# A state-space scan and two mixtures of experts on one core: rows stored once per token, a first stage in written order, and other loads behind the scan

## The chip, the core and the metric

The kernel runs on one core of a Trainium2 chip. Five engines work side by side and wait for one another on semaphores: TensorE (PE, matmuls, with its weight loads shown as PEld), VectorE (DVE), ScalarE (ACT), GpSimd (POOL) and SyncE (SP), which here only issues transfers. Sixteen DMA engines move the data; the queues that feed them belong to SP, ACT and POOL. The metric is the device time of one execution in microseconds (us), lower is better.

## What is computed

x has 8 sequences of 1024 tokens with 256 channels, 8192 tokens in all. Cut to what matters, the reference is:

```python
xn = layernorm(x)
x  = x + scan_block(xn) + routed_experts(xn) + shared_expert(xn)
xn = layernorm(x)
x  = x + attention(xn) + capacity_experts(xn)

def scan_block(x):      # per channel a state of 16: h = A h + Bm x_t; y_t = Cm h + Dm x_t
    return x + gelu(layernorm(y, ln_w, ln_b)) @ W_out.T + b_out
def routed_experts(x):  # 8 experts of width 128, 2 per token, chosen in one of two groups
    # sum over the 2 of  weight * (silu(x @ w_gate) * (x @ w_up)) @ w_down
    ...
def attention(x):       # softmax over the axis of heads; with one head every weight is 1
    # so each token of a sequence gets the same row: the sum of all values, times w_o
    ...
def capacity_experts(x):  # 8 experts of width 1024, 2 per token, at most 2048 tokens per expert
    ...
```

## The kernel before

The work is tiled by 128 tokens (`P`): 64 tiles (`NT`), 8 per sequence (`TPB`), 8 sequences (`NB`). Tensors between the stages lie in DRAM: `xnd` (the normalized rows with the weight of their expert), `base` (x plus normalized x plus shared expert plus b_out), `yr` (what the routed experts give, two rows per token), `xd` (second normalized rows), and the output.

A planner puts the instructions of each engine in an order of its own, by the order in which the code names them as priority, by estimated durations, and by when buffers of a pool come free. The order is fixed when the program is built; each engine then works through its list and waits where an operand is missing. The transfers of SP's and POOL's queues are in such lists too.

**First stage** (lines 457 to 660). For each tile DVE takes mean and variance (`measure`, L553, L554), ACT the root (`scale`, L561), DVE the normalized rows (`normal`, L576). Four tiles of rows make one buffer `xr4` (three buffers), which goes to `xnd` twice, once for each of the two rows that a token has there (L584). `shared` (L596) takes two tiles at a time: PE transposes the rows (`pair_turned`, L249), ACT copies them (L253), PE forms the router's scores (L606) and the shared expert's gate and up products (L263); ACT writes the normalized channels `xc` for the scan and x plus xn into `y` (`both`, L588, L592) and the sigmoid (L268); DVE multiplies (L270, L271), PE goes down (L278), DVE adds the result into `y` (L617). For each sequence `fill` (L535) first writes b_out to all rows of `base`, and POOL adds the finished `y` to it in an accumulating transfer (L655). For every two sequences `route0` chooses the experts (33 small DVE operations) and writes the two weights to `xnd` (L528). The tiles are measured in five sets (1, 2, 2, 2 and 1 sequences), the next set while one is worked on. The eight steps of `krylov(0)` (powers of the first scan matrices) are called two per pair. PE's PSUM buffers are `ps_t` (1), `ps_m` (2), `ps_k` (2, shared by krylov and every second pair's gate/up), `ps_gu` (1), `ps_d` (1).

**Scan and routed experts** (L662 to L902). Eight blocks of channels; under the first two, `find` sorts tokens into 71 expert blocks of 256 rows, `found` (L757) decodes for each row which token and which of its two experts it is; under the other six the blocks run: `bring` gathers rows and weights (L789, L792), `widen` and `narrow` compute, `narrow` scales with the row's weight (L811) and scatters to `yr` (L814).

**Behind the scan** (L905 to L1336). Per sequence: `load(b)` (L942) brings `base` into `hb` (three buffers) and adds the two rows per token of `yr`: for sequence 0 by plain loads into the two buffers `xs` and DVE adds (L959, L961), for the others by two accumulating transfers on POOL's queue (L952), the second behind the first. `turn`, `project` (L988, PE L996, DVE L1003 adds `hb`), `measure`, `normal_out`, `turn_out`, `logits`, `attend`, `route` follow. `attend` (L1071) computes the attention's one row and POOL adds it to all rows of the sequence in the output (L1085). The first two experts' weights `w1t` are loaded in this stage (L909).

**Last experts** (L1339 to L1432). 32 steps of 512 rows: gather (`fetch`, L1362), two layers (PE L1393, L1411), and four scatters per step that add to the output (L1423), each waiting for the one before.

The loop of the first stage that the change rewrites:

```python
for k in range(0, len(g), 2):
    ...
    shared(i, pr, rstd[:, k : k + 2])
    for step in steps[:2]:
        step()
```

Of the kernel before, what the change touches and what calls it, by code (L numbers as in the profile page):

```python
# [9 lines left out]
F32 = mybir.dt.float32  # L10
# [8 lines left out]
P = 128  # L19
EPS = 1e-5  # L20
BIG = 3.0e38


@with_exitstack
def kernel(
# [47 lines left out]
    NCOL = NBLK * BLK // P  # L73
    XW = D + 8
# [10 lines left out]
    kscr = dram.tile([D, 2 * P], F32, name="kscr")  # L85
    base = dram.tile([NTOK, D], F32, name="base")

    xnd = dram.tile([2 * NTOK, D + 1], F32, name="xnd")
# [109 lines left out]
    def pick_two(pool, v, n, hot, val):  # L198


        for k in range(2):
# [6 lines left out]
            nc.vector.tensor_reduce(first, cand, AX.X, ALU.max)  # L208
            oh = hot[k]
            nc.vector.tensor_tensor(oh, cand, bc(first, 2, [P, n, E]), ALU.is_equal)  # L210
            if k == 0:
                rest = pool.tile([P, n, E], F32, name="rest")
                nc.vector.scalar_tensor_tensor(rest, oh, -BIG, v, ALU.mult, ALU.add)
                v = rest


    with tc.tile_pool(name="xpool", bufs=1) as xpool, tc.tile_pool(name="mo", bufs=2) as mo, tc.tile_pool(
# [12 lines left out]
        g0 = xpool.tile([P, 2, NT], F32, name="g0")  # L230
        up = xpool.tile([P, NT], F32, name="up")
        off = xpool.tile([P, NT], F32, name="off")
# [4 lines left out]

        choice = xpool.tile([P, NCOL], I32, name="choice")
        goes = xpool.tile([P, NCOL], I32, name="goes")
# [16 lines left out]
        def hidden(xT, wb, pgu=None):  # L256
# [10 lines left out]
            sg = mo.tile([P, 2 * P], F32, name="sg")  # L267
            nc.scalar.activation(sg, pgu[:, 0, :], AF.Sigmoid)  # L268
            hh = mo.tile([P, 2 * P], F32, name="hh")
            nc.vector.tensor_tensor(hh, pgu[:, 0, :], sg, ALU.mult)  # L270
# [183 lines left out]
        with tc.tile_pool(name="sh", bufs=1) as sh, tc.tile_pool(name="ld", bufs=2) as ld, tc.tile_pool(  # L454
# [5 lines left out]
            scores = sh.tile([P, NT, E], F32, name="scores")  # L460
            cb_t = sh.tile([P, E], F32, name="cb_t")
# [10 lines left out]
            bout_t = sh.tile([P, D], F32, name="bout_t")  # L472
            nc.scalar.dma_start(bout_t, b_out.partition_broadcast(P))
# [6 lines left out]
            nc.vector.tensor_copy(rwT.rearrange("p c e -> p (c e)"), pr[:, : DC * E])  # L480

            def route0(n, tiles):
# [8 lines left out]
                nc.vector.tensor_tensor(lo, v[:, :, 0:2], v[:, :, 2:4], ALU.min)  # L491
                gs = rt.tile([P, 2 * n], F32, name="gs")
                nc.vector.tensor_reduce(gs, lo, AX.X, ALU.max)
                top = rt.tile([P, 2 * n], F32, name="top")
                nc.vector.tensor_reduce(top, hi, AX.X, ALU.min)
                nc.vector.tensor_tensor(gs, gs, top, ALU.max)
                nc.vector.tensor_reduce(top, hi, AX.X, ALU.max)
                nc.vector.tensor_tensor(gs, gs, top, ALU.add)
                gs2 = gs.rearrange("p (t g) -> p t g", g=2)
                gm = rt.tile([P, n, 2], F32, name="gm")  # L500
                nc.vector.tensor_tensor(gm[:, :, 0], gs2[:, :, 0], gs2[:, :, 1], ALU.is_ge)
                nc.vector.tensor_tensor(gm[:, :, 1], gs2[:, :, 1], gs2[:, :, 0], ALU.is_gt)
                masked = rt.tile([P, n, E], F32, name="masked")
# [7 lines left out]
                pick_two(rt, masked, n, hot, [rt.tile([P, n], F32, name=f"top{j}") for j in range(2)])  # L511
                w = rt.tile([P, n, E], F32, name="w")
                nc.vector.tensor_tensor(hot0[:, tiles, :], hot[0], hot[1], ALU.add)
                nc.vector.tensor_copy(first0[:, tiles, :], hot[0])
                nc.vector.tensor_tensor(w, hot0[:, tiles, :], sc, ALU.mult)
                den = rt.tile([P, n], F32, name="den")
                nc.vector.tensor_reduce(den, w, AX.X, ALU.add)
                nc.vector.tensor_scalar(den, den, 1e-20, None, ALU.add)
                nc.vector.reciprocal(den, den)
                nc.vector.tensor_tensor(w, w, bc(den, 2, [P, n, E]), ALU.mult)  # L520
                for k in range(2):
                    wk = rt.tile([P, n, E], F32, name="wk")
                    nc.vector.tensor_tensor(wk, w, hot[k], ALU.mult)
                    nc.vector.tensor_reduce(g0[:, k, tiles], wk, AX.X, ALU.add)
                    mine = xnd[2 * tiles.start * P : 2 * tiles.stop * P, :].rearrange(
                        "(i p k) c -> k p i c", p=P, k=2
                    )[k]
                    nc.sync.dma_start(mine[:, :, D], g0[:, k, tiles])  # L528
# [4 lines left out]
            def fill(b):  # L533

                nc.sync.dma_start(  # L535
                    base[b * S : (b + 1) * S, :].rearrange("(i p) d -> p i d", p=P),
                    bc(bout_t, 1, [P, TPB, D]),
                )

# [31 lines left out]
            def normal(i, mv, rstd):  # L571
# [7 lines left out]
                if i % 4 == 3:  # L579
                    for kk in range(2):  # L580
                        mine = xnd[2 * (i - 3) * P : 2 * (i + 1) * P, :].rearrange(
                            "(i p k) c -> k p i c", p=P, k=2
                        )[kk]
                        nc.sync.dma_start(mine[:, :, :D], rows[i // 4])  # L584
# [10 lines left out]

            def shared(i, pr, rstd):  # L596


                n = i // 2
                pt = None  # L600
                if n % 3:
                    pt = ps_m.tile([P, 512], F32, name="pm").rearrange("p (c t) -> p c t", c=DC)
                xT = pair_turned(rows[i // 4][:, i % 4 : i % 4 + 2, :], pt)
# [11 lines left out]
                pgu = ps_k.tile([P, 2, 2 * P], F32, name="pk") if n % 2 else None  # L615
                pd = down(hidden(xT, sw, pgu), sw)
                nc.vector.tensor_tensor(y[:, i : i + 2, :], pd, y[:, i : i + 2, :], ALU.add)  # L617

# [7 lines left out]
            pr = None  # L626
            for s, g in enumerate(sets):
                mv = mvs[s]
                rstd = scale(g, mv)
                nxt = []  # L630
                if s + 1 < len(sets):
                    nxt = list(sets[s + 1])
                    mvs.append(ld.tile([P, len(nxt), 2], F32, name="mv"))
                for i in g[:4]:
                    normal(i, mv[:, i - g[0], 0:1], rstd[:, i - g[0] : i - g[0] + 1])
                for k in range(0, len(g), 2):
                    for i in g[k + 4 : k + 6]:
                        normal(i, mv[:, i - g[0], 0:1], rstd[:, i - g[0] : i - g[0] + 1])
                    for i in nxt[k * len(nxt) // len(g) : (k + 2) * len(nxt) // len(g)]:
                        measure(i, mvs[s + 1][:, i - nxt[0], :])  # L640
                    i = g[k]
                    if i % TPB == 0:
                        pr = ps_y.tile([P, TPB, E], F32, name="py")
                        fill(i // TPB)
                        if i // TPB >= NB - len(pack):
                            nc.sync.dma_start(*pack[i // TPB - NB + len(pack)])
                    shared(i, pr, rstd[:, k : k + 2])
                    for step in steps[:2]:
                        step()
                    steps = steps[2:]  # L650
                    if i % TPB == TPB - 2:
                        b = i // TPB
                        tiles = slice(b * TPB, (b + 1) * TPB)
                        nc.scalar.activation(scores[:, tiles, :], pr, AF.Sigmoid)
                        nc.gpsimd.dma_start(  # L655
                            base[b * S : (b + 1) * S, :].rearrange("(i p) d -> p i d", p=P),
                            y[:, tiles, :], accum_op=ALU.add,
                        )
# [807 lines left out]
```

## Time and profile before

| what | us |
|---|---|
| median of three runs (2046.37 to 2051.86) | 2048.63 |
| the profiled execution | 2030.81 |
| its span, first to last instruction | 2029.1 |
| PE busy | 1825.1 |
| ACT busy | 716.2 |
| DVE busy | 697.3 |
| POOL busy | 670.8 |
| last add of the shared expert ends (L617) | 203.3 |
| first load behind the scan (L946) | 858.3 |
| first gather of the last experts (L1362) | 1092.5 |

The profile is of one execution. Its page cuts the span into 40 slices of 50.7 us, each digit the busy share in tenths. A timeline line has start, duration, engine, source line, operation, output and inputs, the number of merged instructions, and in brackets how long the engine sat idle and for whom it waited. The chain of work that ended last is followed back from the last instruction. A granted clock of 1.00 is PE at full speed. In the diff, load_first(0) is given the two xs buffers as room, load_first(1) the two w1t buffers.

### The profile page before, as it was taken

To read this page: it belongs to the slowest core of one execution; us is meant where nothing else is said; L and a number is where in the kernel's file an instruction comes from. 1 tells how busy PE (TensorE), PEld (TensorE's weight loads), DVE (VectorE), ACT (ScalarE), POOL (GpSimd) and SP (SyncE) were. 2 spreads that over 40 slices of the span, in tenths; PEclk is the share of its full clock that TensorE was granted. 3 is DMA by queue.
4 is the path that set the end of the run, shared out by engine and by line. 5 is a ranking of instruction groups with operands and counts; after the bars stand their busy time and mean duration, and the time that the engine had idled before them with its cause. 6 is when DMAs were issued, how large, how long until landed. Compare 5 with 4: busy or idle time off the path is not lost.

```text
span 2029.1 us, 24196 instructions
## 1 busy us (share of the span) xinstructions
PE 1825.1 (90%) x8619; PEld 1379.9 (68%) x8619; DVE 697.3 (34%) x2101; ACT 716.2 (35%) x1626; POOL 670.8 (33%) x680
## 2 busy tenths in 40 slices
PE   6988798989898888748995999999999999999996
PEld 5866576877777776537973666666666666666664
DVE  6764795444453434437775111001000110001010
ACT  5963353232222222337982222222222222222221
POOL 0000002555555546411112333333333333333312
PEclk9988899999999999868997999999999999999998
DMA  9999313555454545499995223232323222232211
GB/s 267 222 199 201 49 54 115 151 149 152 146 164 138 146 130 170 122 281 253 224 237 128 38 60 61 42 72 39 82 39 73 41 61 57 57 59 38 40 18 21
DMA packets 228888, 233.16 MB, mean 115 GB/s; under 512 B 50904, under 2 KB 203296, under 8 KB 228640
## 3 DMA queue, kind: packets, MB, share of 16 engines
q0 software_dynamic: 69408, 102.87, 26.2%
q1 hardware_dynamic: 156672, 126.35, 22.5%
q10 hardware_dynamic: 2688, 2.40, 0.4%
q8 instruction: 68, 1.11, 0.2%
q14 instruction: 52, 0.43, 0.1%
HBM read 136.87 MB, written 97.85 MB: 116 GB/s over the span
## 4 chain that ended last, share of the span: by engine, by line
PE 48%; DMA 4%; issue 2%; DVE 2%; ACT 1%; POOL 1%; POOLq 0%; SPq 0%; DVEq 0%; ACTq 0%
PE phe L1393 22%; PE poe L1411 21%; DMA hb<-yr 2%; PE px L1376 1%; PE pd L996 1%; PE pd L1061 1%; DMA hb<-base 1%; PE pt L933 1%; DMA out_dram<-yo,invi 1%; PE pi L1162 0%; PE pt L1206 0%; PE pt L1042 0%; DVE y L1003 0%; DVE st L178 0%; POOL out_dram L1085 0%
## 5 line engine op out<-in xcount | busy, mean ns | idle before, releaser
L1393 PE MATMUL phe<-xTe,w1t 128*128 128x512 f32 x1024 | 447.1, 595 | 0.6 <-issue 0.6
L1411 PE MATMUL poe<-w2t,hT 128*128 128x256 f32 x2048 | 447.3, 379 | 0.0
L1411 PEld LDWEIGHTS poe<-w2t,hT 128*128 128x128 f32 x2048 | 386.7, 190 | 51.7 <-issue 0.5
L1393 PEld LDWEIGHTS phe<-xTe,w1t 128*128 128x128 f32 x1024 | 195.4, 191 | 233.6 <-issue 230.5
L1423 POOL DMA_INDIRECT out_dram<-yo,invi x128 | 201.6, 1575 | 447.7 <-DMA out_dram<-yo,invi 257.2
L1400 ACT ACTIVATE hT<-phe,b1T 128x512 f32<-128x512 f32 x256 | 175.9, 687 | 248.3 <-PE phe L1393 241.4
L1422 ACT ACTIVATE yo<-yo,gr 128x256 f32<-128x256 f32 x128 | 58.0, 500 | 441.4 <-DVE yo L1418 441.4
L1418 DVE TENSOR_TENSOR yo<-poe,b2t 128x512 f32<-128x512 f32 x64 | 44.2, 691 | 406.6 <-PE poe L1411 406.6
L1362 POOL DMA_INDIRECT xg<-xd,invi x128 | 124.0, 969 | 163.8 <-PE px L1376 125.8
L322 PE MATMUL pk<-kr 128*128 128x129 f32 (+7 forms) x896 | 151.4, 306 | 29.4 <-ACT kr L333 23.8
L1377 DVE COPY xTe<-px 128x512 f32<-128x512 f32 x64 | 41.2, 685 | 383.3 <-PE px L1376 383.2
L322 PEld LDWEIGHTS pk<-kr 128*128 128x128 f32 x896 | 130.1, 202 | 52.9 <-ACT kr L333 34.5
L814 POOL DMA_INDIRECT yr<-yo,goes x142 | 140.7, 990 | 76.7 <-DVE yo L811 35.2
L792 POOL DMA_INDIRECT xb<-xnd,choice x142 | 139.1, 980 | 46.9 <-issue 33.5
L263 PE MATMUL pgu<-xT,wb 128*128 128x256 f32 x568 | 144.2, 399 | 8.9 <-ACT xT L253 7.6
L263 PEld LDWEIGHTS pgu<-xT,wb 128*128 128x128 f32 x568 | 110.3, 200 | 37.4 <-ACT xT L253 18.5
L333 ACT COPY kr<-pk 128x256 f32<-128x256 f32 x192 | 69.6, 374 | 123.4 <-DVE kr L329 103.5
L268 ACT ACTIVATE sg<-pgu 128x256 f32<-128x256 f32 x87 | 33.3, 383 | 199.7 <-PE pgu L263 139.3
L278 PE MATMUL pd<-wb,hh 128*128 128x256 f32 x284 | 86.4, 421 | 11.4 <-DVE hh L271 7.6
L787 POOL COPY wb<-wrow 1x1 int32<-1x1 int32 x71 | 12.8, 180 | 234.4 <-PE pgu L752 117.5
L270 DVE TENSOR_TENSOR hh<-pgu,sg 128x256 f32<-128x256 f32 x87 | 36.8, 423 | 138.8 <-ACT sg L268 116.1
L996 PE MATMUL pd<-woutT,gT 128*128 128x256 f32 x256 | 63.5, 404 | 22.1 <-DVE y L1003 22.1
(322 smaller groups left out, 2375.3 us busy)
## 6 DMA issues: line engine op xcount, KB each, us to landing
wb<-wpk SPq DMA_DIRECT2D x71, 384.0 KB
xnd<-xr SPq DMA_DIRECT2D x32, 512.0 KB
hk<-kscr SPq DMA_DIRECT2D x32, 512.0 KB
hb<-yr POOLq DMA_DIRECT2D x14, 1024.0 KB
base<-bout_t SPq DMA_DIRECT2D x8, 1024.0 KB
base<-y POOLq DMA_DIRECT2D x8, 1024.0 KB
hb<-base SPq DMA_DIRECT2D x8, 1024.0 KB
w1t<-in_L_ffn_w_dram SPq DMA_DIRECT2D x8, 1024.0 KB
```

Source lines behind the costliest of these rows:

```text
L263: nc.tensor.matmul(pgu[:, j, :], lhsT=gu[:, j, c, :], rhs=xT[:, c, :], start=(c == 0), stop=(c == DC - 1),)
L278: nc.tensor.matmul(pd[:, q, :], lhsT=hh[:, q * P : (q + 1) * P], rhs=wb[:, 2 * DC * I : WW], start=True, stop=True,)
L322: nc.tensor.matmul(pk[:, j, :n], lhsT=t[:, 1 - j, P:], rhs=t[:, j, P - k : P - k + n], start=True, stop=True,)
L333: nc.scalar.copy(t[:, :, P:], pk[:, :, k : k + P])
L792: nc.gpsimd.indirect_dma_start(out=xb[:, q, : D + 1], out_offset=None, in_=xnd[:, :], in_offset=bass.IndirectOffsetOnAxis(ap=choice[:, 2 * ...
L814: nc.gpsimd.indirect_dma_start(out=next(yr_own)[:, :], out_offset=bass.IndirectOffsetOnAxis(ap=goes[:, 2 * n + q : 2 * n + q + 1], axis=0) ...
L996: nc.tensor.matmul(po[:, q, :], lhsT=gT[:, c, (t + q) * P : (t + q + 1) * P], rhs=woutT[:, c, :], start=(c == 0), stop=(c == DC - 1),)
L1362: nc.gpsimd.indirect_dma_start(out=xg[:, q, :], out_offset=None, in_=xd[:, :], in_offset=bass.IndirectOffsetOnAxis(ap=invi[:, q0 + q : q0 ...
L1393: nc.tensor.matmul(ph, lhsT=w1t[:, c, h * P : (h + 1) * P], rhs=xT[:, c], start=(c == 0), stop=(c == DC - 1),)
L1400: nc.scalar.activation(hT[:, h], ph, AF.Relu, bias=b1T[:, e * HC + h : e * HC + h + 1])
L1411: nc.tensor.matmul(po[:, r, :], lhsT=hT[:, h, q + r, :], rhs=w2t[:, h, :], start=(h == 0), stop=(h == HC - 1),)
L1423: nc.gpsimd.indirect_dma_start(out=of[:, :], out_offset=bass.IndirectOffsetOnAxis(ap=invi[:, q0 + r : q0 + r + 1], axis=0), in_=yo[:, r, : ...
```

## The change

*Rows.* `xnd` holds one row per token: 256 channels and both weights (258 numbers). The rows are written once. The routed experts' gather takes the whole row; `found` keeps in `which` which of the two weights is meant, and `narrow` picks it with a multiplication and a sum and adds half of b_out to each of a token's two rows (`bhalf`). So `fill` goes, and `base` is written by plain transfers of four tiles from SP's queue instead of accumulated.

*Written order.* In the first stage PE, DVE and ACT run in the order of the code. The code is staggered: transposes one pair ahead, the way down one pair behind, rows two pairs ahead, krylov's steps one every second pair, `route0` cut into pieces of which three run per pair. At a set's end, `begin(s + 1)` (root, scalings, four tiles of rows of the next set) stands ahead of the last pair's own work.

*Behind the scan.* Sequences 0 and 1 are loaded plainly, sequence 1's two halves into the buffers of `w1t`, and DVE adds them (`add_first`, two tiles at a time); `load(2)` is called at once. `attend` leaves its row in `y`, and POOL adds it to the output after one of the first eight steps of the last experts.

The diff, cut to its core:

```diff
+IN_ORDER = {mybir.EngineType.PE, mybir.EngineType.DVE, mybir.EngineType.Activation}
+    XR = D + 2
-    xnd = dram.tile([2 * NTOK, D + 1], F32, name="xnd")
+    xnd = dram.tile([NTOK, XR], F32, name="xnd")
...
+        bhalf = xpool.tile([P, D], F32, name="bhalf")
+        nc.scalar.dma_start(bhalf, b_out.partition_broadcast(P))
+        nc.scalar.mul(bhalf, bhalf, 0.5)
+        which = xpool.tile([P, NCOL, 2], BF16, name="which")
...
-            sg = mo.tile([P, 2 * P], F32, name="sg")
-            nc.scalar.activation(sg, pgu[:, 0, :], AF.Sigmoid)
-            hh = mo.tile([P, 2 * P], F32, name="hh")
-            nc.vector.tensor_tensor(hh, pgu[:, 0, :], sg, ALU.mult)
+            hh = mo.tile([P, 2 * P], F32, name="hh", bufs=3)
+            nc.scalar.activation(hh, pgu[:, 0, :], AF.Sigmoid)
+            nc.vector.tensor_tensor(hh, pgu[:, 0, :], hh, ALU.mult)
...
-                    for kk in range(2):
-                        mine = xnd[2 * (i - 3) * P : 2 * (i + 1) * P, :].rearrange(
-                            "(i p k) c -> k p i c", p=P, k=2
-                        )[kk]
-                        nc.sync.dma_start(mine[:, :, :D], rows[i // 4])
+                    mine = token_rows(slice(i - 3, i + 1))
+                    nc.sync.dma_start(mine[:, :, :D], rows[i // 4])
...
+            def add_shared(i, hh):
+                pd = down(hh, sw)
+                nc.vector.tensor_tensor(y[:, i : i + 2, :], pd, y[:, i : i + 2, :], ALU.add)
+                if i % 4 == 2:
+                    nc.sync.dma_start(
+                        base[(i - 2) * P : (i + 2) * P, :].rearrange("(i p) d -> p i d", p=P),
+                        y[:, i - 2 : i + 2, :],
+                    )
...
+            with tc.manual_schedule(engines=IN_ORDER):
+                begin(0)
+                turn(0)
+                pr, back = None, None
+                routes = {2 * TPB: 0, 4 * TPB: 2 * TPB, 6 * TPB: 4 * TPB, 7 * TPB: 6 * TPB, 8 * TPB: 7 * TPB}
+                routing = iter(())
+                for s, g in enumerate(sets):
+                    ...
+                    for k in range(0, len(g), 2):
+                        for i in g[k + 4 : k + 6]:
+                            mean, rstd, j = scale_of[i]
+                            normal(i, mean, rstd[:, j : j + 1])
+                        for i in nxt[k * len(nxt) // len(g) : (k + 2) * len(nxt) // len(g)]:
+                            measure(i, mvs[s + 1][:, i - nxt[0], :])
+                        if nxt and k == len(g) - 2:
+                            begin(s + 1)
+                        i = g[k]
+                        ...
+                        if i + 2 < NT:
+                            turn(i + 2)
+                        rstd = scale_of[i][1]
+                        hh = shared(i, pr, rstd[:, k : k + 2])
+                        if back:
+                            add_shared(*back)
+                        back = i, hh
+                        if i // 2 % 2 and steps:
+                            steps.pop(0)()
+                        for _ in range(3):
+                            next(routing, None)
+                        if i + 2 in routes:
+                            for _ in routing:
+                                pass
+                            routing = route0(i + 2 - routes[i + 2], slice(routes[i + 2], i + 2))
+                add_shared(*back)
...
+                gk = mo.tile([P, 2, 2], F32, name="gk")
+                tc.keep_in_program_order(nc.vector.tensor_tensor(
+                    gk, xb[:, :, D:XR], which[:, 2 * n : 2 * n + 2, :], ALU.mult
+                ))
+                gs = mo.tile([P, 2], F32, name="gs")
+                nc.vector.tensor_reduce(gs, gk, AX.X, ALU.add)
                 yo = eb_.tile([P, 2, D], F32, name="yo", bufs=2)
                 for q in range(2):
-                    nc.vector.tensor_scalar(
-                        yo[:, q, :], pd[:, q, :], xb[:, q, D : D + 1], None, ALU.mult
+                    nc.vector.scalar_tensor_tensor(
+                        yo[:, q, :], pd[:, q, :], gs[:, q : q + 1], bhalf, ALU.mult, ALU.add
                     )
...
+        def load_first(b, room):
+            hb = xr.tile([P, TPB, D], F32, name="hb")
+            nc.sync.dma_start(hb, base[b * S : (b + 1) * S, :].rearrange("(i p) d -> p i d", p=P))
+            parts = []
+            for h in range(2):
+                yk = room[h].rearrange("p (i k d) -> p i k d", k=2, d=D)
+                nc.sync.dma_start(yk, stored(b)[:, h * TPB // 2 : (h + 1) * TPB // 2])
+                parts.append(yk)
+            hold[b] = hb
+            return parts
+        def add_first(b, parts):
+            hb = hold[b][0] if isinstance(hold[b], tuple) else hold[b]
+            for t in range(0, TPB, 2):
+                at = t % (TPB // 2)
+                for j in range(2):
+                    nc.vector.tensor_tensor(
+                        hb[:, t : t + 2, :], hb[:, t : t + 2, :],
+                        parts[t * 2 // TPB][:, at : at + 2, j, :], ALU.add,
+                    )
...
-            at = rt.tile([P, D], F32, name="at")
-            nc.scalar.copy(at, pa[:, :D])
-            mine = of[b * S : (b + 1) * S, :].rearrange("(i p) d -> p i d", p=P)
-            nc.gpsimd.dma_start(mine, bc(at, 1, [P, TPB, D]), accum_op=ALU.add)
+            nc.scalar.copy(y[:, b * TPB, :], pa[:, :D])
...
-        load(0)
-        load(1)
+        firsts = [load_first(0, ...), load_first(1, ...)]
+        load(2)
         turn(0)
         measure_scan(0)
+        add_first(0, firsts[0])
...
                 roots(b)
+                if b == 0:
+                    add_first(1, firsts[1])
...
+                if n <= NB:
+                    nc.gpsimd.dma_start(
+                        of[(n - 1) * S : n * S, :].rearrange("(i p) d -> p i d", p=P),
+                        bc(y[:, (n - 1) * TPB, :], 1, [P, TPB, D]), accum_op=ALU.add,
+                    )
```

## Prediction

> **What bounds the kernel now.** I read the page's slices, then stretches of the span, the queues' shares, the chain, and the timelines of PE, DVE, ACT and POOL. Slices first:
>
> ```profile
> PE   6988798989898888748995999999999999999996
> DVE  6764795444453434437775111001000110001010
> ACT  5963353232222222337982222222222222222221
> DMA  9999313555454545499995223232323222232211
> ```
>
> Four stages: the first (slices 1 to 4, DMA full), scan and experts (PE 8 to 9, the others half idle), behind the scan (DMA full again), the last experts (PE 9 throughout). In the first, by stretches (busy PE, PEld, DVE, ACT, POOL; clock; DMA share; GB/s):
>
> ```profile
> 100.00:121.00 21.00, 20.40 (x122) 18.00 (x122) 16.46 (x65) 18.91 (x34) 1.54 (x1) 1.00 0.97 174
> 121.00:140.00 19.00, 14.01 (x58) 11.14 (x57) 7.45 (x23) 13.64 (x25) 1.54 (x1) 0.73 0.96 190
> 140.00:160.00 20.00, 11.50 (x61) 9.32 (x59) 14.65 (x50) 4.62 (x11) 1.54 (x1) 0.82 1.04 236
> 160.00:180.00 20.00, 19.12 (x83) 16.33 (x83) 4.79 (x11) 5.27 (x12) 0.00 (x0) 0.75 0.97 195
> ```
>
> To 121 us PE is full; then it waits, and its clock falls. The queues of 0 to 215 us (packets, MB, share of 16 engines):
>
> ```profile
> q1 hardware_dynamic: 67232, 37.08, 67.4%
> q0 software_dynamic: 8320, 8.39, 26.3%
> ```
>
> 67.4% of 215 us is 145 us (3.9 us per MB), 26.3% is 57 us for the 8.39 MB accumulated into base (6.7 per MB): 202 of 215 us. DMA bounds the stage's end. Behind the scan, the chain:
>
> ```profile
> 872.84 14.91 DMA hb<-yr
> 888.03 19.08 DMA hb<-yr
> 907.21 0.70 DVE y L1003
> ...
> 1024.57 14.49 DMA hb<-yr
> 1039.15 0.69 DVE y L1003
> ```
>
> Sequence 1's two accumulating loads run one behind the other; DVE sits from 881.6 to 907.2 (its waits list 28.7 us on hb<-yr, twice).
>
> **First stage, traffic.** Out go 16 of 32 xnd writes, 8 fills (8.4 MB each) and 8 accumulates (8.4 MB); in come 16 plain base writes (8.4 MB). 37.1 - 8.4 MB at 3.9 us is 112 us, against 202: DMA is no bound any more, and the stalls on row buffers (DVE xr, 7.0 us at 157) go. Next late is PE. One pair of tiles, start to start at 185.8 to 191.5: 8 gate/up matmuls 1.81, router 0.81, down 0.87, transposes 0.43: 3.92 us. Twelve pairs were left at 121; 47 us of work took 82 (the last add ends at 203.3). At most 35 us are to be had.
>
> **First stage, written order.** Per pair ACT needs 3.0 us (two xc and two y 2.2, xT 0.5, sigmoid 0.3) and DVE 2.7 to 4.5 (normals 0.65, moments 0.8, hh 0.66, add 0.6, route pieces up to 1.8): inside a set PE stays the bound, since down(k-1) stands behind gate/up(k) and rows are made two pairs ahead. Not so at the four set boundaries. There begin(s+1) stands ahead of turn(i+2), and PE, in order, holds the router, gate/up and down work behind transposes that need the new set's rows. From the end of the previous pair on PE, DVE must finish hh (0.4), the add (0.6), nine route operations (0.2 each, 1.8), two moments (0.8), then ACT's square root (0.3), reciprocal and two scalings (0.5), two rows (0.65): 5.1 us. The first boundary has four moments and no route (4.2), the last one moment (4.7): 19 us together. And idleness has a second price:
>
> ```profile
> 119.32 1.97 PE L263 MATMUL pk<-xT,sw 128*128 128x256 f32 x8
> 121.13 1.03 PE L278 MATMUL pd<-sw,hh 128*128 128x256 f32 x4
> 125.39 1.80 PE L278 MATMUL pd<-sw,hh 128*128 128x256 f32 x4 [3.23 <-DVE hh L271]
> ```
>
> After 3.23 us idle the same four matmuls take 1.80 us instead of 1.03, and PE stays at half speed to 136. Half-speed stretches last 5.6 us (from 862.3), 6.75 (908), 10.7 (125), 12.5 (157); half is lost: 2.8 to 6.2. I take 3.3, since nothing else stalls PE behind a boundary, as at 908: 13 us. [...]
>
> krylov(0): a level is 16 matmuls, 2.2 us; in order its third and fourth group wait on two PSUM buffers that DVE empties behind hh and the add: 2.7. Seven levels and a start of 4 (3.2 at 199.5): 23 us. Sum: first transposes 20.5, half-clock start 4.5 (to 29.6), 32 x 3.92 = 125.4, 23, 19, 13, drain 3 (sigmoid, hh, down, add): 208, against 203.3: **+5**. Bounds: without stops and half clock, with levels at 2.2: 170 (-33); with 12.5 us stretches (+12), and krylov(1), whose first 7 us ran inside the old tail (199.5 to 206.8), behind the stage: +24. The last route chain is 33 shorter operations behind the last add; its hot0 came 3.1 us behind the add and does again: 0. bhalf's scaling on ACT lies before 9.3 us, where ACT idles; uncovered 0.5.
>
> **Scan.** Each of 71 blocks gains two small DVE operations (0.2 each); the two yo take one more SBUF operand (0.48 now; DVE's two-operand PSUM form is 0.42). DVE is 20 to 22 of 50 us busy there beside PE's 44 to 46, so 0; uncovered, 0.4 x 71 = 28 us, which needs PE to wait on yo, and its idle time there ends on kr, xT or hh. found and the gather keep their counts. The planner reorders this stage anew: +-5.
>
> **Behind the scan.** Sequence 0 keeps its 3 MB; eight adds of 0.6 replace four of 1.2: 0. Sequence 1's 3 MB follow on SP: 6 MB at 3.0 us per MB (359 GB/s in 860 to 870) from 858.8 land by 879. add_first(1) fits where DVE idles from 881.6; the first y add moves from 907.2 to 883: -24. ACT, which used that wait for xs, y and xT to 892, then has 17 us per sequence and, 9.2 to 10 of 10 busy in 980 to 1040, sets the pace; project(2) could begin at 900 instead of 923. But sequence 2: its base load was already issued at 859.97 beside sequence 1's, so "at once" moves nothing; it lands at 881 behind 2 MB more, and two accumulates follow at 6.25 us of engines' time per MB (66.1% of 858 to 1048 for 20.08 MB), shared with plain traffic 11 us each: ready at 903, or 913 if sequence 3's first comes between. I take 5 us back. Six attend accumulates leave the stage (6 x 6.25 us): the 3.1 us wait at 1039 goes. -24 + 5 - 3 = **-22**. Bounds: -10 (ready at 913, clock lost again) to -30 (no new wait, and the attend traffic's cut felt). The first w1t loads wait for add_first(1) and are used at 1100: covered by 200 us, uncovered 6.
>
> **Last experts.** Eight accumulates of 1 MB enter POOL's queue behind four scatters per step. Those run 4.6 us apart (1183.1 to 1196.9), ending at 1201; the next gathers start at 1203, used at 1230; the next scatter at 1211.5. The old stage's last accumulate, issued at 1082.85, had the engines busy to 1092, some 9 us. 18.4 + 9 fits the 28.4 us step: 0. Behind a waiting accumulate stand the gathers, with some 19 us to spare; only then would PE wait. If it took 15 us: 8 x 6 - 19 = 29 us.
>
> **Sum:** +5 - 22 = -17 on 2030.8 us (span 2029.1). The runs' median, 2048.6, is 18 above the profiled execution; the difference is carried over: **2032**.
>
> **Rivals.** *PE runs through the first stage:* if the moments arrive early enough, the end is at 170: -33 - 22 = -55, 1994. For it: PE full to 121 with the same work. Against: the order at the boundaries. *Sequence 2's accumulates take the place of sequence 1's:* ready at 913, -10 + 5 = -5, 2044. For it: 15 and 19 us per accumulate now. *Written order stops PE longer* (slower): at four boundaries PE idles 5 us and runs 12.5 at half clock, and krylov(1) comes behind: +24, with -10 at the back +14, 2063. It decides once the last shared add ends later than about 225. For it: 12.5 us at 157; against: 6.75 at 908. *It doesn't do what it says:* true of the third's load, priced above at nothing.
>
> **Chances.** Forecast 0.45 (2017 to 2043); PE through 0.27; sequence 2 0.13; longer stops 0.15. A measurement tells 0.3%, 6 us. Faster: 0.45 + 0.27, less 0.02 of the forecast's edge, 0.70; within: 0.13 + 0.02; slower: 0.15. The range runs from the second case, 1992, to past the third, 2054; longer stops are left out.
>
> **What would show it.** DMA share in 100 to 200 us well under 0.9; four PE gaps of 4 to 5 us with a DVE xr as releaser, each with half clock behind; last add near 208. Behind the scan no 25 us wait; a first y add of sequence 1 some 25 us after the stage's first load, and 0 to 12 us of waiting on hb<-yr for sequence 2. Last stage: PE without idle time. I am wrong if the gaps are missing (then faster), if the last add is late, or if steps with accumulates grow beyond 28.4 us.

## The result, and the profile after

The change made the kernel slower: 2069.45 us median of five runs, against 2050.09 for the kernel before beside it; ratio 1.0084, 95% interval 1.0062 to 1.0106, some 17 us. Measured again later it was 1.0106 (1.0073 to 1.014). I had forecast 2032 and a gain of 17.

The kernel before took 2050, 2033, 2049 and 1966 us beside the four sets of runs in this study (the last three sets were on one chip each, and on three different ones), so kernels of different sets are compared by their ratio to it, or by those stages of the profile that did not vary.

The slices of the kernel after, which answer to those of before (with the granted clock):

```profile
PE   5788799888889798768895999999999999999996
DVE  4666797343434344464878101100101010011000
PEclk8988899999999999988898999999999999999998
DMA  8233213454444445559963246544323222232211
```

DMA has fallen from 9 to 2 or 3 in the first stage, as worked out, and PE is no fuller there than it was. By stretches (busy PE, PEld, DVE, ACT, POOL; clock; DMA share; GB/s), and the traffic of the first 235 us:

```profile
100.00:121.00 21.00, 18.96 (x96) 16.59 (x96) 12.59 (x42) 13.76 (x26) 0.00 (x0) 0.80 0.31 81
140.00:160.00 20.00, 12.44 (x56) 10.40 (x55) 13.53 (x51) 12.05 (x21) 0.00 (x0) 0.74 0.41 133
```
```profile
q1 hardware_dynamic: 51448, 28.70, 43.1%
```

28.7 MB are what I had counted; the 8.4 accumulated MB are gone. 43.1% of 235 us is 101 us of engine time, against 202 of 215 before. Still PE idles and runs at half clock in between, and no engine is full.

Behind the scan, the chain:

```profile
916.35 15.09 DMA hb<-base
931.44 0.30 issue
931.74 1.69 POOL hb L1006
...
970.82 14.32 DMA hb<-yr
```

The wait on the second sequence's accumulating loads is gone; the third's base load now stands behind 6 MB of plain loads on SP's queue, POOL issues its accumulates at 931.7 and 944.5, and DVE waits for them:

```profile
962.47 0.69 DVE L1068 TENSOR_TENSOR y<-pd,hb 128x512 f32<-128x512 f32 x1 [12.76 <-DMA hb<-yr]
```

Stage by stage, from profiles (us). The last two columns run from the first load behind the scan to the last experts' first gather, and from there to the end:

| kernel, order of its first stages | last shared add | first scatter | first to last scatter | behind the scan | last experts |
|---|---|---|---|---|---|
| before | 203.3 | 344.4 | 510.8 | 234.2 | 936.6 |
| back_only (as before) | 208.0 | 349.6 | 516.4 | 225.4 | 933.4 |
| two_small_ops (as before) | 206.7 | 348.0 | 529.0 | 232.2 | 937.3 |
| third_ahead (as before) | 209.9 | 351.5 | 443.8 | 223.1 | 933.3 |
| after | 223.0 | 359.1 | 545.4 | 226.2 | 935.8 |
| after_again | 223.9 | 360.9 | 544.0 | 224.2 | 936.1 |

The order of before has its last shared add at 203 to 210, mean 207, and its first scatter at 348; after is 16 later at the one and 12 at the other. Behind the scan it gains 8, in the last experts 1. The rest is in the scan stage, which I had priced at nothing: beside runs of before at 2049 us, 544 against 529, 15 us. 12 + 15 - 8 - 1 = 18, beside 19 and 20 by the medians. (Only this scan stage varies from set to set; see the end. Each number is of one execution: turn_behind, below, has the code of after in this stage and took 552 in the same set.)

My theory at this point: the written order costs the first 12; in the scan stage POOL's order of gathers and scatters costs most of the 15; and the third sequence's accumulates take back most of what the second's plain load wins. Rivals: the 15 are chance; the small weight operations themselves cost it; the first stage is slow for its new structure, not its order.

### The profile page after: what moved, and what is told of

It reads as the page before. It is cut to its first block, busy times and chain, and to the rows that moved or that the text cites. A ratio compares the mean times of both kernels' runs of the same rounds, so it can differ in the third digit from the quotient of the medians.

```text
span 2069.3 us, 24369 instructions
## 1 busy us (share of the span) xinstructions
PE 1839.1 (89%) x8619; PEld 1394.5 (67%) x8619; DVE 730.5 (35%) x2289; ACT 731.8 (35%) x1628; POOL 661.9 (32%) x670
## 4 chain that ended last, share of the span: by engine, by line
PE 47%; DVE 2%; DMA 2%; issue 2%; ACT 1%; POOL 0%; SPq 0%; POOLq 0%; DVEq 0%; ACTq 0%
PE phe L1468 21%; PE poe L1486 21%; PE px L1451 1%; PE pd L1061 1%; DMA hb<-base 1%; DMA hb<-yr 1%; DMA out_dram<-yo,invi 1%; PE pt L988 1%; PE pd L1126 1%; DVE hl L1210 1%; DVE hh L1215 0%; ACT y L193 0%; SPq L1016 0%; PE pi L1225 0%; PE pt L1269 0%
## 5 line engine op out<-in xcount | busy, mean ns | idle before, releaser
L1437 POOL DMA_INDIRECT xg<-xd,invi x128 | 124.8, 975 | 195.2 <-PE px L1451 87.8
L279 ACT ACTIVATE hh<-pgu 128x256 f32<-128x256 f32 x87 | 33.1, 381 | 209.3 <-PE pgu L274 92.2
L280 DVE TENSOR_TENSOR hh<-pgu,hh 128x256 f32<-128x256 f32 x87 | 36.8, 423 | 148.4 <-ACT hh L279 116.2
L866 DVE SCALAR_TENSOR_TENSOR yo<-pd,gs,bhalf 128x256 f32<-128x256 f32 x142 | 62.1, 479 | 55.6 <-PE pd L288 36.0
```

The source lines that it names most:

```text
L866: nc.vector.scalar_tensor_tensor(yo[:, q, :], pd[:, q, :], gs[:, q : q + 1], bhalf, ALU.mult, ALU.add)
L1437: nc.gpsimd.indirect_dma_start(out=xg[:, q, :], out_offset=None, in_=xd[:, :], in_offset=bass.IndirectOffsetOnAxis(ap=invi[:, q0 + q : q0 ...
```

## The experiments

### The back part alone (back_only)

The kernel before with the diff's parts behind the scan and in the last experts, nothing else.

> The kernel before with the part behind the scan alone (plain loads of two sequences, the third begun at once, attend's accumulates moved into the last experts); first stage and scan keep the order of before on every engine. My theory, from after's trace (stage from the first load behind the scan to the first gather of the last experts 225.8 us against 234.2): 8 us faster than before, 2042; last shared add at 203 and the blocks of the scan stage unchanged, so its profile also shows how far stage two differs between two executions of one order. Rival (the back part gains nothing by itself, since what it saves at sequence 1 returns at sequences 2 and 3): within 3 us of before. Rival (moved accumulates hold up the last experts): last stage over 940 us.

Measured: ratio 0.9953 (0.993 to 0.9975), 9.6 us faster than before; stage 225.4 against 234.2. So this part of the change gains: as expected here, and under half of the 22 us that the prediction gave it. The last experts take no longer with the eight accumulates. From the stage's first load, the sequences' first y adds begin at 11, 27, 54, 77 and 115 us (before: 11, 49, 67, 84 and 121). The second wins 22, the third 12, the fourth 7, the fifth 6.

### The third's load ahead (third_ahead)

```
             ]),
+            load(2),
             load_first(1, [ ... ]),
-        load(2)
```

> The kernel before with the back part alone, and in it the third sequence's load (base, then its two accumulating loads) issued ahead of the second's plain loads, no longer behind them. In that part the sequences began 11, 27, 54 and 77 us into the stage (before: 11, 49, 67, 84): 22 us gained at the second, 7 at the fourth, 9 in the end. If the late start of the third's accumulating loads (issued at 24, behind 6 MB) is what gives the gain back: second at 32 to 36, third at 42 to 47, fourth at 65 to 70, stage 218 to 222, 3 to 7 us faster than the back part alone. Rival (the accumulating loads of the following sequences pace the stage whenever they start): fourth at 75 or later, stage 224 to 228, the same time.

```profile
847.05 0.69 DVE L1013 TENSOR_TENSOR y<-pd,hb 128x512 f32<-128x512 f32 x1 [5.26 <-DMA hb<-yr]
872.70 0.69 DVE L1013 TENSOR_TENSOR y<-pd,hb 128x512 f32<-128x512 f32 x1 [11.09 <-DMA hb<-yr]
```

These are the third's and the fourth's first adds, 48.7 and 74.3 us into the stage (54.4 and 77.0 in back_only). The third's wait shrank from 12.3 to 5.3 us, and the fourth's grew from 5.4 to 11.1. Stage 223.1, ratio 0.9949 (0.9933 to 0.9966), not to be told from back_only's 0.9953. The rival's numbers (75 and 224) are met within 1 us: the accumulating loads, two per sequence one behind the other, pace the third and fourth in both runs, begun behind the 6 MB or ahead of them.

### The planner's order in the first stage (planner_front)

```
-            with tc.manual_schedule(engines=IN_ORDER):
+            if True:
```

> After, without the written order: the planner orders PE, DVE and ACT in the first stage, everything else as after (one row per token, base written once by plain stores). My theory (the order written out stops PE at four boundaries and at each krylov level, traffic is no bound any more): the last shared add falls from 221.9 to between 170 and 195, and the kernel is 25 to 50 us faster than after, 2020 to 2044, so it beats before. Rival (the code's structure, with transposes one pair ahead and the add one pair behind, is what is slow, or the moments are): the last add stays between 210 and 222 and the time within 10 us of after.

Measured: ratio 1.0031 (1.0011 to 1.0051), against after's 1.0084: 11 us faster than after (15 by after's later ratio, 1.0106), not 25 to 50, and 6 us slower than before (its scan stage took 532 us, with POOL's order as in after). Last shared add 201.2. So the written order costs 22 us at that point, and the planner's order with half the DMA engine time ends only 6 us ahead of the planner's order with all of it (its code is also staggered, so the 6 are not the traffic's alone). So the traffic was not what held the stage. What did, PE's timeline, the stretch and DVE's timeline show:

```profile
150.57 1.23 PE L260 MATMUL pt<-ident,xr 128*128 128x128 f32 x4 [7.06 <-DVE xr L588]
```
```profile
140.00:160.00 20.00, 11.81 (x46) 9.49 (x44) 12.09 (x42) 6.35 (x13) 0.00 (x0) 0.66 0.37 118
```
```profile
149.91 0.28 DVE L546 TENSOR_REDUCE g<-wk 128x16 f32<-128x128 f32 x1
150.11 2.02 DVE L588 TENSOR_SCALAR xr<-y,mv,rstd 128x256 f32<-128x256 f32 x6
```

The same stop of 7 us on the rows xr as before had at 157, again with half clock behind it, at a DMA share of 0.37. DVE was not waiting: from 142 to 150 it ran the routing of 16 tiles, and the rows came behind. With this in mind, the timelines of the kernel before, DVE then PE:

```profile
156.80 0.28 DVE L524 TENSOR_REDUCE g<-wk 128x16 f32<-128x128 f32 x1
157.00 2.66 DVE L576 TENSOR_SCALAR xr<-y,mv,rstd 128x256 f32<-128x256 f32 x8
```
```profile
157.46 1.23 PE L249 MATMUL pt<-ident,xr 128*128 128x128 f32 x4 [7.00 <-DVE xr L576]
```

It was there already: L524 is the last operation of the routing. I had seen the 7.0 us and the full queues and put the one down to the other without asking what DVE did meanwhile. And of the waits that before's profile lists between 20 and 215 us, none of PE, ACT or DVE ends on a DMA.

The other long stop of before, 3.23 us at 122 with half clock (0.50) from 126 to 136, is not a routing chain. It ended on hh, whose sigmoid on ACT stood behind the square root for the next set, with a table load ahead of each:

```profile
121.03 1.28 ACT L561 ACT_TABLE_LOAD   x1
122.33 0.30 ACT L561 ACTIVATE rstd<-mv,epst 128x8 f32<-128x8 f32 x1
122.65 1.28 ACT L268 ACT_TABLE_LOAD   x1
123.94 0.38 ACT L268 ACTIVATE sg<-pk 128x256 f32<-128x256 f32 x1
```

No run was made against that one.

### Routing pinned (route_pinned), beside its base (planner_combo)

planner_combo is planner_front with the weight operations of gs_in_xb_pin below. route_pinned issues each routing operation through a helper that pins it behind what DVE was given before it:

```
+    class Pinned:
+        def __getattr__(self, op):
+            return lambda *a: tc.keep_in_program_order(getattr(nc.vector, op)(*a))
...
```

> After with the planner's order in the first stage and the weight operations in spare columns of xb, pinned (POOL's order as in before). If the parts add up as the profiles had them (last add 201 instead of 222, scan stage 13 us shorter, behind the scan as in after): ratio to before 0.995 to 0.998, that is 5 to 10 us faster than before and as good as the back part alone. Rival (the scan stage's order differs again with what stands in front of it): over 1.002.

> The run before, with each routing operation of the first stage pinned behind the DVE instructions traced before it, so that the planner can't run a whole routing chain ahead of the next rows. In the planner's order PE stopped 7.1 us at 150 and 5.3 us at 178, each time while DVE ran 21 to 33 routing operations ahead of the rows, with the DMA share at 0.1 to 0.4. My theory (these chains, and not traffic, were what stopped PE, in before too): both stops go, the clock stays near 1.0 in 140 to 180, last shared add at 185 to 192, 8 to 15 us faster than the run beside it. Rival (moments or ACT stop PE there, the routing only fills the gap): stops of 4 us and more stay, last add 198 to 204.

planner_combo: 0.9946 (0.9929 to 0.9964), at the lower edge of what was expected; it beats both kernels, by as much as the back part alone (0.9953). route_pinned: 0.9936 (0.9915 to 0.9956), last shared add 195.5 against 201.5. The stops at 150 and 178 (7.0 and 5.3 us) became:

```profile
148.53 1.22 PE L264 MATMUL pt<-ident,xr 128*128 128x128 f32 x4 [2.79 <-DVE xr L592]
```

and 3.06 at 172.8, while one at 114 grew from 1.94 to 4.36. So the chains were over half of the one stop and under half of the other; what is left of them is not the routing alone. 6 us at the last add, not 10 to 16, and in time no more than the interval: the direction is shown, the size is half.

### Transposes behind at the set boundaries (turn_behind)

```
-                        if i + 2 < NT:
+                        late = nxt and k == len(g) - 2
+                        if i + 2 < NT and not late:
                             turn(i + 2)
 ...
                             add_shared(*back)
+                        if late:
+                            turn(i + 2)
```

> After, with one change: at the four set boundaries the next pair's transposes stand behind this pair's router, gate/up and the previous pair's down on PE, no longer ahead of them. My theory (the first stage's 18 us over before are the boundary gaps, 24.8 us of idle PE, and the half clock behind them): gaps fall to 1 to 3 us each, the last shared add from 222 to between 185 and 200, and the time by 20 to 35 us against after. Rival (krylov's levels in order and the chain through ACT and DVE pace the stage, gaps merely move): last add over 212, less than 10 us gained.

Measured: ratio 1.0117 (1.0082 to 1.0151), the same as after's 1.0106 in the same set; last add 224.3. My theory failed here. After's four stops were 4.50, 6.65, 7.57 and 6.03 us (at 46, 101, 154, 194). Around the second, PE of after and of turn_behind:

```profile
101.17 1.22 PE L260 MATMUL pt<-ident,xr 128*128 128x128 f32 x4 [6.65 <-DVE xr L588]
```
```profile
85.85 0.73 PE L332 MATMUL pk<-kr 128*128 128x136 f32 x4 [1.51 <-DVE hh L281]
...
101.23 1.23 PE L260 MATMUL pt<-ident,xr 128*128 128x128 f32 x4 [2.36 <-DVE xr L588]
105.76 3.39 PE L332 MATMUL pk<-kr 128*128 128x144 f32 x12 [2.35 <-DVE hh L281]
```

One stop became two, here and at the other boundaries; together they still stop PE for 19.6 us, of 24.8. At 101 the rows come no earlier than before, only PE has more to do until then; and ACT's square root for the new set, which waits for DVE's moments to 99.97, stands ahead of this pair's sigmoid, with four scalings and a table load of 1.28 us between, so the sigmoid starts at 104.4, the product hh follows, and krylov's level with it. The clock fell to half here from 101 to 115 (in after: 98 to 108), and once more from 88 to 95, where after had none (see the end). From 20 to 220 us PE's busy time rose from 165.8 to 172.1 us and its mean clock fell from 0.89 to 0.86: idle time was traded for half-clock time.

### No routing ahead of a boundary (route_aside)

The run with both mends (combo, below), and no routing piece in the iteration ahead of a boundary:

```
-                        for _ in range(3):
+                        for _ in range(0 if nxt and k == len(g) - 4 else 3):
                             next(routing, None)
```

> Written order as in the run that had both mends, and besides no routing piece in the iteration ahead of a set boundary (nine DVE operations, 2.6 us, that stood between the last rows' moments and PE's next transposes). There the transposes' move had cut the gaps from 24.8 to 9 us and left the last add at 222, with the half-clock stretch behind 101 us grown from 10 to 13 us. My theory (short stops keep the clock at half as long ones do; only no stop helps): if the rest of the stops at 101, 154 and 196 falls under 1 us, last add 200 to 210 and 10 to 18 us gained; if stops of 2 us stay, 218 to 222 and under 4 us gained. Rival (idle time alone counts): 2 to 7 us gained whatever the clock.

Measured: ratio 1.0016 (1.0001 to 1.0031), last add 214.8, against combo's 1.0052 and 221.9: 7 us both by the ratios (of two sets) and at the last add. The stop at 101 went, but a krylov level behind it waits 3.17 us on hh; at 147 to 151 and 189 to 196 pairs of stops of 1.2 to 2.6 us stay. This lies between the two cases of the theory and at the upper edge of the rival's, so it does not separate clock from idle time. Written order is still 13 us behind the planner's 201.5 there.

### POOL's order in the scan stage (gs_in_xb, gs_in_xb_pin, combo)

In after the last reader of a gathered block is the small pair of operations gk and gs, not the scaling yo. The planner therefore lets POOL issue the gather of block n+3 ahead of the scatters of block n: in before, copy, two scatters, two gathers repeat 68 times; in after gathers stand on both sides of the copy and ahead of the scatters. POOL's and DVE's timelines in after:

```profile
378.06 0.98 POOL L869 DMA_INDIRECT yr<-yo,goes  x1 [0.30 <-issue]
385.68 1.00 POOL L839 DMA_INDIRECT xb<-xnd,choice  x1 [6.64 <-DVE gs L863]
386.68 0.18 POOL L834 COPY wb<-wrow 1x1 int32<-1x1 int32 x1
```
```profile
385.16 0.17 DVE L339 COPY kr<-pk 128x16 f32<-128x16 f32 x1 [1.32 <-PE pk L332]
385.25 0.15 DVE L859 TENSOR_TENSOR gk<-xb,which 128x4 f32<-128x4 f32 x1
```

The gather waits 6.6 us for gs; gk is pinned behind krylov's copies, which wait for PE; and behind the gather stand the next weights' copy and this block's scatters. gs_in_xb puts gk and gs into spare columns of xb, so that the scaling is again the last reader, and drops the pin; gs_in_xb_pin keeps it:

```
-                gk = mo.tile([P, 2, 2], F32, name="gk")
+                gk = xb[:, :, D + 2 : D + 4]
                 tc.keep_in_program_order(nc.vector.tensor_tensor(gk, ...))
-                gs = mo.tile([P, 2], F32, name="gs")
+                gs = xb[:, :, D + 4]
...
-                        yo[:, q, :], pd[:, q, :], gs[:, q : q + 1], bhalf, ALU.mult, ALU.add
+                        yo[:, q, :], pd[:, q, :], xb[:, q, D + 4 : D + 5], bhalf, ALU.mult, ALU.add
```

> After, with the block's two small weight operations writing into spare columns of xb, unpinned, so that the scaling is again the last reader of xb. This gives POOL the order of before: copy, two scatters, two gathers; in after the planner had put gathers of block n+3 ahead of the scatters of block n. My theory (this order costs, since the gather waits for the weight operations and holds the scatter and the next weights' copy behind it): first to last scatter falls from 545 us to 511 to 525, time 7 to 20 us under after, 2049 to 2062. Rival (the 34 us between the two profiles are chance of the execution or the planner's reshuffle on PE, DVE and ACT): the same time as after within 4 us, and a stage of 535 to 550.

> As the run before, but the first weight operation stays pinned to its place in the written order, as in after. POOL again has the order of before. If POOL's order is the cause: as the run before, 7 to 20 us under after. If the pin is (DVE's operations around it are held in order): no more than 3 us under after, and the stage from first to last scatter stays above 535.

gs_in_xb: ratio 1.0524, some 107 us slower than before, with POOL's old order; first to last scatter took 616 us, where 511 to 525 were expected. Its waits tell why:

```profile
DVE xb L859 <- DMA xb<-xnd,choice: 241.9, 62, 7.5
```

Without the pin the planner puts the next block's product ahead of the work at hand, and DVE stops in order until the gather lands, 3.9 us on the mean. So the pin, the other cause I had weighed, is a needed guard, and this run says nothing on POOL's order.

gs_in_xb_pin: 1.0059 (1.0035 to 1.0083), scan stage 526.5, some 5 to 10 us better than after by the ratios. The clean comparison is within one set. combo is turn_behind with these lines, and nothing else differs:

> After with both mends: transposes behind at the boundaries, and the weight operations in spare columns of xb, pinned. If the two parts add up: last add 185 to 200, scan stage 520 to 527, behind the scan 225, so 25 to 40 us under after and 8 to 22 under before (2011 to 2025 where before is 2033); about that of the kernel before with the back part alone (2023), or better. Rival: the gain of the first stage is lost in the scan stage, since krylov(1) and the finds then meet the same DVE: equal to before.

combo 2057.87 us (1.0052), turn_behind 2071.36 (1.0117): 13.5 us, and first to last scatter 532 against 552. The sums expected of the first stage did not come, since turn_behind brought nothing. POOL's waits in turn_behind, then in combo:

```profile
POOL xb L842 <- DVE gs L866: 50.7, 21, 6.5
POOL yr L872 <- DVE yo L869: 26.2, 14, 12.6
```
```profile
POOL yr L872 <- DVE yo L869: 59.7, 49, 12.8
```

The gathers' waits on gs are gone; POOL waits for yo instead, where nothing but the next gathers, with blocks in hand, stand behind. So these lines, which give POOL its old order, are shown to be worth most of the 15 us: of the 13.5, 2.6 are there at the first scatter (359.7 and 357.1), which leaves 11 for the scan stage. (The 20 us between the two stages are more, but turn_behind's profiled execution took 7 us more than its median.) They are not POOL's order alone: with them the planner also moved 52 of DVE's 2289 operations and 15 of PE's 8619 matmuls. ACT's order is the same.

### The small operations by themselves (two_small_ops), and after once more (after_again)

two_small_ops adds to before a product and a sum of that size per block, the first pinned; PE, ACT and POOL keep their order.

```
                 pd = down(hh, wb)
+                gk = xb[:, :, D + 2 : D + 4]
+                tc.keep_in_program_order(nc.vector.tensor_tensor(
+                    gk, xb[:, :, D - 1 : D + 1], xb[:, :, D - 1 : D + 1], ALU.mult
+                ))
+                nc.vector.tensor_reduce(xb[:, :, D + 4], gk, AX.X, ALU.add)
```

> The kernel before with two more small DVE operations per block (a product and a sum of four numbers per partition into spare columns of xb, the first pinned; nothing reads them), all else in the order of before. In the kernel after, the scan stage stayed 9 to 13 us above before even with POOL's old order. If these 142 operations, 0.15 us each and pinned, are the reason: 8 to 14 us slower than before, first to last scatter 522 to 527. Rival (they hide, as I predicted; the shared tile for sigmoid and product, or the planner's other order, is the reason): within 3 us, 511 to 517.

Ratio 1.0011 (0.9988 to 1.0034): no difference that can be told, at most 7 us. Its scan stage of 529 beside before's 2049 us is what after's 544 is to be held against. By the ratio before's own stage, of which this set has no profile, would lie some 2 us below 529. So the two operations hide, as I had said, to within these 7 us.

> The kernel after unchanged, on the same chip as the runs beside it, since its first profile and that of before come from chips that differ (the kernel before had a median of 2050 beside the one and 2033 beside the runs above). Theory: ratio to before 1.008 again, so near 2050; its last shared add near 222 and first to last scatter 530 to 546, where the pinned kernel with POOL's old order took 526.5. Rival (the stage's 545 us were that one execution): 515 to 525.

Ratio 1.0106, scan stage 544.0, last add 223.9: not chance.

## Why the prediction was wrong, point by point

- **The steps that failed, by size:** the forecast was -17 and the stages gave +18. Of the 35 between them the scan stage, put at nothing, is 15; the stage behind the scan, -8 for -22, is 14; the first stage, +12 for +5, is 7; the last experts give 1 back.
- **"DMA bounds the stage's end"**: wrong. The forecast takes no gain from it, but the 35 us "to be had" and the rival at 1994 rest on it. 202 of 215 us of engine time is a sum, not a wait. planner_front halved it under the planner and gained 6 us at the last add, not up to 35: the stop of 7 us was a routing chain ahead of the rows on DVE, the one of 3.23 us a sigmoid behind table loads on ACT. "The stalls on row buffers go" is the same slip.
- **First stage +5**: +16 at the last add, +12 at the first scatter. The mechanism was right: four stops, released by DVE xr, each with half clock behind it. The terms were small: the stops took 24.8 us, not 19; two pairs with a krylov level 11.4 us apart, not 7.84 + 2.7 = 10.5, some 6 over seven levels; PE ran at half clock for some 8, 7, 6 and 6 us behind the stops (the granted clock was 0.50 for 10.2, 10.2, 10.2 and 6.8 us, from before each stop's end), half of it lost, 13 as I had taken. With these 12 of the 15 us between 208 and 223 are placed, and the other 3 are not; the whole is within the bound I had named (+24). I set the forecast near the low end although each shortfall pointed the same way.
- **Scan stage 0**: +15. I priced DVE's operations, which hide. I did not ask which instruction frees xb and what POOL, in order, has behind the one that waits for it. My "planner reorders this stage anew: +-5" had no row behind it. Of the 15, combo shows some 11 for the lines that restore POOL's order. With them, and the planner or the written order in front, the stage took 448 to 451 against third_ahead's 444 in the same set, 526.5 against back_only's 516 and 532 against two_small_ops's 529 in theirs: 3 to 10 us stay, for which I have no cause.
- **Behind the scan -22**: -8 in the stage, -9.6 alone. "First y add of sequence 1 some 25 us after the stage's first load": 27. "Ready at 903, or 913": that is 45 or 55 us into the stage; it came at 55. That is my second rival, at its time and near its price (-10). I took 5 us back and should have carried the wait on to the fourth sequence: the gains run 22, 12, 7, 6.
- **Last experts 0**: -1, PE without idle time there; the eight accumulates are covered, as worked out.

What happened lies between forecast and slower rival in the first stage (the last add came at 223, that rival's at 225 or later, and its stretches of 12.5 us did not come), is my second rival behind the scan, and in the scan one cost that I had no case for. That the slower rival's sum, +14, comes near the measured +17 to +20 is luck: it has nothing for the scan.

## What to carry to other kernels

A full queue beside an idle engine is not yet a cause: look at what the engine that released the wait was doing during it. Here DVE was busy with the routing, and the planner's order with half the DMA engine time ended 6 us earlier at the last add. When an operation is put between a gather and its use, ask which instruction is now the last reader of the buffer, for that decides where the planner puts the next gather in an in-order queue, and what stands behind it: here a gather waited 6.6 us for gs, with the weights' copy and the scatters behind it. And follow a gain through the following stages of a pipeline: a transfer made early for one step showed the next step's transfer as the pace here, with 22 us gained at the second sequence and 8 at the end.

The best version here is the planner's order in the first stage with pinned routing, weight operations in spare columns of xb, and the back part: 0.9936 of before (0.9915 to 0.9956). It can't be told from the same without the pinned routing (0.9946), nor from the back part alone in the kernel before (0.9953).

## What the runs showed of the hardware that I had not expected

**The clock fell behind a short stop in one run, and not behind its like in another.** In turn_behind a stop of 1.51 us, with one of 0.35 just behind, was followed by half clock (0.50); PE, and stretches of 2 us (same columns as above):

```profile
85.85 0.73 PE L332 MATMUL pk<-kr 128*128 128x136 f32 x4 [1.51 <-DVE hh L281]
86.93 1.41 PE L332 MATMUL pk<-kr 128*128 128x136 f32 x8 [0.35 <-ACT kr L343]
```
```profile
84.00:86.00 2.00, 0.49 (x4) 0.29 (x4) 1.90 (x7) 0.00 (x0) 0.00 (x0) 1.00 0.54 193
86.00:88.00 2.00, 1.65 (x12) 1.45 (x13) 0.82 (x4) 0.78 (x3) 0.00 (x0) 0.94 0.21 74
88.00:90.00 2.00, 2.00 (x12) 2.00 (x11) 1.49 (x7) 1.43 (x4) 0.00 (x0) 0.50 0.00 0
94.00:96.00 2.00, 2.00 (x13) 1.74 (x12) 1.21 (x3) 1.64 (x2) 0.00 (x0) 0.85 0.00 0
```

By the mean clocks of 0.94 and 0.85 it fell at 87.8 and was back at 94.6, 6.8 us later, with PE busy for 8 of the 8 us from 88 to 96. In after two stops of 1.52 and 0.35 us at the same place left the clock at 1.00, where it stayed until 98:

```profile
88.32 0.73 PE L332 MATMUL pk<-kr 128*128 128x136 f32 x4 [1.52 <-DVE hh L281]
89.41 1.19 PE L332 MATMUL pk<-kr 128*128 128x136 f32 x8 [0.35 <-ACT kr L343]
```

So here the length of the stop did not decide alone; what did was not shown.

**One stage varied, the others didn't.** In the same order of instructions up to there, first to last scatter took 516 us in back_only and 444 in third_ahead, while their last adds (208, 210), the stage behind the scan (225, 223) and the last experts (933, 933) agree within 2.3 us. The difference goes with the set, which was on another chip: the stage took 444 to 451 us in all four profiles of the set at 1966 us, and 511 to 552 in all others but gs_in_xb. Between 350 and 790 us, ACT's idle time that the profile puts down to "issue" and "remote", that is to nothing it shows on this core, is 39 us in back_only and nil in third_ahead. That can be no more than part of the 72 us; what holds the engines up there wasn't tried and stays open.
